# An attention kernel's inner loop and tail: row maxima taken one by one, two sums joined, one head's row scores issued ahead, GpSimd relieved of two sums, one bias moved

## The chip, the cores and the metric

The kernel runs on one core of one Trainium2 chip. The metric is the device time of one execution in microseconds (us), as the median of several runs. The engines named here are PE (TensorE, with PEld for its weight loads), DVE (VectorE), ACT (ScalarE), POOL (GpSimd) and SP (SyncE, which issues DMAs).

## The reference

Eight batches of 512 rows with 512 features, 16 heads of 32. A condition vector per batch is projected with the same weights and added to Q and K; then comes plain softmax attention, and the input is added as a residual. All is float32.

```python
Q, K, V = (split_heads(x @ W.T + b) for W, b in ((Wq, bq), (Wk, bk), (Wv, bv)))
cQ = Q + split_heads(tokens @ Wq.T + bq)        # tokens: one condition row per batch
cK = K + split_heads(tokens @ Wk.T + bk)
attn = softmax(cQ @ cK^T / sqrt(32))
out = x + merge_heads(attn @ V)
```

## The kernel before

**The steps.** The work is cut into T = 32 steps; step `t` is one batch and one group of four heads (`b, g = divmod(t, 4)`). For each step the scores are made twice. *Row scores* (`row_scores`, L641) have 128 query rows on the partitions and 512 keys along the row, one PSUM bank a head; DVE takes each row's maximum from them (`one_max`, L589, for one head; `row_max_of`, L650, for two heads whose banks are neighbours), and ACT makes the exponentials with the maximum as bias and their sum (`denominators`, L701). For two of the four query blocks of a step these exponentials are kept and turned (`turn_kept`, L660 on DVE; `swap_kept`, L682, DMAs on the queues of SP and POOL). For the other two blocks, the *rest*, the transposed scores are made anew: `exponentials_of_rest` first puts the maximum into the bank by a bf16 matmul with ones (L774), then adds the rest scores (L785), and ACT takes the exponential (L795).

**The loop.** `thirds(t)` is called for t = 1 to 28 and works in three parts. At its start it makes the row scores of step t+1, query blocks 1 and 2 (`row_max_aside`, `row_max`): head 0's bank of block 1 is copied aside by ACT (L628) and its maximum taken from there (L637), the other three maxima from the banks. Then PE multiplies step t-1's exponentials by V (`weighted`, L816), and makes one item of the projections of a coming batch (`one_item`). Parts i = 1 and i = 2 each make one half of the rest of step t, the row scores of one block of a later step (block 3 of step t+1, then block 0 of step t+2), and one more item. An odd t makes Q first, Q other, K first; an even t V first, K other, V other. The projections are done with seven block products in place of eight, all in `product` (L461), so each item ends in sums that put the products together: `first_by_others` (Q and K first), `other_products` (Q and K other; L551, L486 on DVE), `first_of_v` (copies by ACT, L1217 and L1218) and `other_shared` (V other; L1202 on ACT, L1204 to L1206 on DVE, L1208 on POOL).

**Order and banks.** PE, ACT, DVE and POOL run in the order in which the code is written; nothing is reordered by a planner on them. The eight PSUM banks go round: `begin` and `released` keep a list of them by the time of their release, and `banks(i)` is the i-th of the list. A matmul that writes a bank waits until the bank's last reader is done. `begin` also sorts a neighbouring pair to the end of a group of four, so that the two last heads can share one maximum.

**Row strips.** Head j lies on partitions 32j to 32j+31, so the four heads' scores use four different strips of 32 rows of TensorE. Projections and the products with V use strips of 32 columns.

**The tail.** From t = 29 on the code is written out. It splits the row maxima of step 30 into three bf16 parts on DVE (`split_max`, L715 to L718), turns them on PE (`transpose_max`, L737), and goes on with `crossed` (L1270, L1273), in which row scores and transposed scores alternate. `bias_residual` (L204) is a POOL sum that adds V's bias to the residual of a step; the tail calls it for steps 31, 29 and 30.

Of the kernel before, what the change touches and what calls it, by code (L numbers as in the profile page):

```python
# [17 lines left out]
def kernel(  # L18
# [38 lines left out]
    nc = tc.nc  # L57
# [451 lines left out]
    def first_by_others(n, b, u, dens, at, last, mixed):  # L509

        one_, two_ = halves(banks(at[0])), halves(banks(at[1]))
        c1, c12, c2, c22 = parts_of(n, b, u)
        product(n, b, u, 1, one_[:, 0])
        product(n, b, u, 7, one_[:, 1])
        product(n, b, u, 6, two_[:, 1])
        product(n, b, u, 2, two_[:, 0], (0,))
        if mixed:
            dens((0, 1))
            nc.scalar.copy(c2, one_)
            dens((2, 3))  # L520
            nc.vector.tensor_tensor(c1, two_, twice(c2[:, 0, :]), ALU.add)
            last()
        else:
            dens((0, 1))
            if mixed is False:
                dens((2, 3))
            if mixed is None:
                dens((2, 3))
                nc.vector.tensor_copy(c2, one_)
                nc.vector.tensor_copy(c1, two_)  # L530
            else:
                nc.scalar.copy(c2, one_)
                nc.scalar.copy(c1, two_)
            last()
            nc.gpsimd.tensor_tensor(c12, c12, c2[:, 0, :], ALU.add)
            nc.gpsimd.tensor_tensor(c22, c22, c12, ALU.add)
            nc.gpsimd.tensor_tensor(c1[:, 0, :], c1[:, 0, :], c2[:, 0, :], ALU.add)
            return
        nc.gpsimd.tensor_tensor(c22, c22, c12, ALU.add)
# [48 lines left out]
    def one_max(t, qc, j, pt):  # L588
        nc.vector.tensor_reduce(  # L589
            nmax[t][:, qc, j : j + 1, 0], pt, AX.X, ALU.max, negate=True  # L590
        )

    def row_max(t, qc, hold=False, w=HG):

        if t >= T:
            return
        open_max(t)
        for j in range(HG):
            row_scores(t, qc, j, banks(w + j))
        if row_of[0] or t < T - 2 or t * NS + qc == T * NS - 1:  # L600
            for j in range(2):
                one_max(t, qc, j, banks(w + j))
        else:
            row_max_of(t, qc, 0, banks(w, 2))
        last, both = [banks(w + 2), banks(w + 3)], banks(w + 2, 2)
        apart = row_of[0] and row_of[0][w + 3] - row_of[0][w + 2] > 1

        def held():
            if apart or hold and t < T - 2:
                for j in range(2):  # L610
                    one_max(t, qc, 2 + j, last[j])
            else:
                row_max_of(t, qc, 1, both)

        if hold:
            return held
        held()
        return nothing
# [4 lines left out]
    def row_max_aside(t, qc):  # L623

        open_max(t)
        for j in range(HG):
            row_scores(t, qc, j, banks(j))
        nc.scalar.copy(spare, banks(0).rearrange("p (c f) -> p c f", f=P))  # L628
        one_max(t, qc, 1, banks(1))
        if row_of[0][3] - row_of[0][2] > 1:  # L630
            for j in (2, 3):
                one_max(t, qc, j, banks(j))
        else:
            row_max_of(t, qc, 1, banks(2, 2))

    def max_aside(t, qc):
        nc.vector.tensor_reduce(nmax[t][:, qc, 0:1, 0], spare, AX.XY, ALU.max, negate=True)  # L637
# [11 lines left out]
    def row_max_of(t, qc, pr, pt):  # L649
        nc.vector.tensor_reduce(  # L650
            nmax[t][:, qc, pr * 2 : pr * 2 + 2, 0], pt, AX.X, ALU.max, negate=True
        )
# [112 lines left out]
            for i in range(2):  # L765
                nc.scalar.activation(e[:, i, :], bank[pr * 2 + i], AF.Exp)

    def exponentials_of_rest(t, half):

        bank = [banks(i) for i in range(HG)]  # L770
        rest = slice(KQ * P, S)
        for j in range(HG):
            r = slice(j * HD, j * HD + 3)
            nc.tensor.matmul(  # L774
                bank[j],
                onesb[r, :],
                maxT[t][r, rest].unsqueeze(1).broadcast_to([3, 2, HS]),
                start=True,
                stop=False,
            )  # L780
        for i in range(2):
            kc = half * 2 + i
            for j in range(HG):
                r = slice(j * HD, (j + 1) * HD)
                nc.tensor.matmul(  # L785
                    bank[j][:, i * HS : (i + 1) * HS],
                    qkT["k", t][r, kc * P : (kc + 1) * P],
                    qkT["q", t][r, rest],
                    start=False,
                    stop=(i == 1),  # L790
                )
        for pr in range(NP):
            e = es[t, half, pr] = store[:, 12 + half * 2 + pr]
            for i in range(2):
                nc.scalar.activation(e[:, i, :], bank[pr * 2 + i], AF.Exp)  # L795

    def times_v(t, kc, pt, chunks=range(NS)):
        b, g = divmod(t, G)
# [330 lines left out]
    def thirds(t, made):  # L1129

        b, r = divmod(t, G)
        of = (t - 1) // G + 1
        begin(0, HG)
        turn_more(t, 0, 0)
        row_max_aside(t + 1, 1)
        max_aside(t + 1, 1)
        row_max(t + 1, 2, False, HG)
        turn_more(t, 0, 1)
        denominators(t + 1, 1, None, (1, 2, 3, 0))
        denominators(t + 1, 2, HG)  # L1140
        weighted(t - 1, banks(0), banks(1), nothing)
        turn_more(t, 0, 2)
        load_blocks()
        one_item(of, *next(made), (2, 3), ignore, nothing)
        released(0, 1, 4, 5, 6, 7, 2, 3)
        for i in (1, 2):
            begin(HG)
            exponentials_of_rest(t, i - 1)
            turn_more(t, i, 0)
            rows = (t + 1, 3) if i == 1 else (t + 2, 0)  # L1150
            row_max(*rows, False, HG)
            turn_more(t, i, 1)
            if i == 1:
                first = range(6 if t + 1 < KEPT[-1] else 3)
                swap_kept(t, 2, first)
                split_max(t + 1)
                turn_max(t + 1)
                swap_kept(t, 2, range(len(first), 6))
            dens = lambda js=range(HG): denominators(*rows, HG, js)
            n, u, kind = next(made)  # L1160
            if kind == "first":
                products(of, n, u, kind, False, dens, nothing, None)
                turn_more(t, i, 2)
            elif n == "v":
                small = nothing
                if t + 1 not in KEPT:
                    small = lambda: transpose_max(t + 1, banks(2), nc.scalar.copy)
                other_shared(of, n, u, dens, (0, 3), small, lambda: turn_more(t, i, 2))
                released(1, 2, 4, 5, 6, 7, 0, 3)
            else:  # L1170
                products(of, n, u, kind, False, dens, nothing, False)
                turn_more(t, i, 2)
            if i == 1:
                aparts[t] = masked(t)
            load_blocks()
            if (t + 1, i) == (KEPT[-1], 1):
                swap_kept(t + 1, 0)
            if i == 2:
                if r == 0:
                    combine_x(b + 1, 1, nc.gpsimd)  # L1180
                load_residual(t + 1)
            else:
                if t > 1:
                    bias_residual(t)
                if r == 0:
                    combine_x(b + 1, 0, nc.gpsimd)
            if i == 2 and t + 1 < KEPT[-1]:
                for move in range(2):
                    swap_kept(t + 1, move)

    def other_shared(b, n, u, dens, at, small, more):

        dens((0, 1))
        one_, two_ = banks(at[0]), banks(at[1])
        product(n, b, u, 4, one_[:, :HS])
        product(n, b, u, 5, one_[:, HS:])
        small()
        product(n, b, u, 2, two_[:, :HS])
        product(n, b, u, 3, two_[:, HS:])
        c1, c12, c2, c22 = parts_of(n, b, u)  # L1200
        m45 = aside[:, 0]
        nc.scalar.copy(m45, halves(one_))  # L1202
        dens((2, 3))
        nc.vector.tensor_tensor(c12, one_[:, HS:], c12, ALU.add)  # L1204
        nc.vector.tensor_tensor(c1[:, 0, :], two_[:, :HS], c2[:, 0, :], ALU.add)
        nc.vector.tensor_tensor(c12, two_[:, HS:], c12, ALU.add)  # L1206
        more()
        nc.gpsimd.tensor_tensor(c2, m45, twice(c22), ALU.add)  # L1208

# [97 lines left out]
    else:  # L1307
        row_max_of(t + 1, 2, 1, banks(HG + 2, 2))
    row_max_of(t + 1, 2, 0, late[0][:, :2, :])
    swap_kept(t, 1)  # L1310
    apart = masked(t - 1)
    aparts[t] = masked(t)
    load_residual(t + 2)
    bias_residual(t + 2)
    swap_kept(t, 2)
    bias_residual(t)
    load_residual(t + 1)
    halves_of(t - 1, banks(0), (1,))
    row_of[0] = [*second[:2], *first[2:], *first]
# [152 lines left out]
```

## Time and profile before

| | |
|---|---|
| runs | 653.80, 654.09, 654.63 us (median 654.09) |
| profiled execution | 656.53 us, span 654.7 us, mean granted TensorE clock 0.997 of full speed |
| PE busy | 647.7 us (99%) |
| DVE busy | 598.4 us (91%) |
| ACT busy | 534.3 us (82%) |
| POOL busy | 428.6 us (65%) |
| loop (t = 1 to 28) | from 66.2 to 606.7 us |

The profile comes from one execution; the span runs from its first to its last instruction. A busy PE need not be PE at its peak, since matmuls are pipelined and one that waits inside can count as busy. Rows of the timeline give start, duration, engine, line, operation, what is written from what, the shape, the count, and in brackets the idle time before and what ended it.

### The profile page before, as it was taken

Reading aid. Unit: us, or ns where it says so; the run is one execution under the profiler, and the core shown is the slowest. Engines: PE = TensorE matmul, PEld = TensorE weight load, DVE = VectorE, ACT = ScalarE, POOL = GpSimd, SP = SyncE. Lnnn points to the kernel's source line nnn. Section 1 sums busy time; section 2 is a strip of 40 time slices with the busy share of each in tenths; the row PEclk is TensorE's granted clock in tenths of the full one; section 3 lists DMA queues with packets and bytes.
Section 4 is the critical chain, followed back from the end, with each engine's and each line's share of the span. In section 5 each row is a group of like instructions: output and inputs, shape, how many; then the busy total and the mean of one; then the engine's idle time right before and its main releaser. Section 6 shows DMA issues by size and latency. Waiting matters only on the chain. (4 is left out here: it accounts for less than half of the span.)

```text
span 654.7 us, 24917 instructions
## 1 busy us (share of the span) xinstructions
PE 647.7 (99%) x9856; PEld 350.3 (54%) x9856; DVE 598.4 (91%) x833; ACT 534.3 (82%) x1364; POOL 428.6 (65%) x679
## 2 busy tenths in 40 slices
PE   9999999999999999999999999999999999999997
PEld 8445555555555555555555555555555555555442
DVE  3799999999999999999999999999999989899877
ACT  2479888889888888988888988888898888898464
POOL 3643656786766786777657786668767676766550
PEclk9999999999999999999999999999999999999999
DMA  7633588889877887877877888788987767797811
GB/s 188 107 49 61 127 170 181 172 167 183 185 154 173 163 183 168 185 179 160 173 173 155 188 181 169 165 172 174 171 187 175 149 148 165 147 170 159 190 34 33
DMA packets 248457, 102.02 MB, mean 156 GB/s; under 512 B 229962, under 2 KB 230474, under 8 KB 248340
## 3 DMA queue, kind: packets, MB, share of 16 engines
q1 hardware_dynamic: 234196, 65.54, 53.8%
q0 software_dynamic: 12384, 33.83, 19.2%
q8 instruction: 78, 1.28, 0.9%
q10 hardware_dynamic: 1760, 1.05, 0.5%
q14 instruction: 39, 0.32, 0.2%
HBM read 19.75 MB, written 8.39 MB: 43 GB/s over the span
## 5 line engine op out<-in xcount | busy, mean ns | idle before, releaser
L701 ACT ACTIVATE store<-psum,nmax 128x512 f32<-128x512 f32 x204 | 140.0, 701 | 36.1 <-DVE nmax L589 26.3
L701 ACT ACTIVATE psum<-psum,nmax 128x512 f32<-128x512 f32 x248 | 164.7, 669 | 3.6 <-DVE nmax L589 3.0
L589 DVE TENSOR_REDUCE nmax<-psum 128x1 f32<-128x512 f32 x225 | 144.5, 679 | 18.9 <-PE psum L641 16.6
L650 DVE TENSOR_REDUCE nmax<-psum 128x2 f32<-128x1024 f32 x125 | 151.5, 1212 | 0.0
L641 PE MATMUL psum<-kT,qT 32*128 32x512 f32 x1024 | 143.2, 619 | 0.0
L795 ACT ACTIVATE store<-psum 128x512 f32<-128x512 f32 x232 | 119.8, 603 | 26.9 <-PE psum L785 26.9
L682 POOL DMA_DIRECT2D store<-store x258 | 128.3, 503 | 18.1 <-DMA store<-store 9.3
L660 DVE STREAM_TRANSPOSE store<-store 128x1024 f32<-128x1024 f32 x116 | 138.9, 1217 | 0.0
L816 PE MATMUL psum<-store,v 128*32 128x256 f32 x1856 | 107.6, 383 | 0.0
L816 PEld LDWEIGHTS psum<-store,v 128*32 128x32 f32 x1856 | 57.2, 110 | 57.5 <-ACT wT_q L628 21.2
L889 POOL TENSOR_TENSOR res<-res,recs 128x512 f32<-128x512 f32 x30 | 31.3, 1045 | 84.5 <-DVE res L888 84.5
L641 PEld LDWEIGHTS psum<-kT,qT 32*128 32x128 f32 x1024 | 56.0, 184 | 35.7 <-issue 19.6
L785 PE MATMUL psum<-qT,kT 32*128 32x256 f32 x928 | 59.9, 373 | 0.0
L701 ACT ACTIVATION_READ_ACCUMULATOR psum<-psum,nmax 128x1 f32 x248 | 52.9, 213 | 0.0
L461 PE MATMUL psum<-wc_v,xc 128*32 128x256 f32 x768 | 47.7, 379 | 0.0
L785 PEld LDWEIGHTS psum<-qT,kT 32*128 32x128 f32 x928 | 45.5, 184 | 4.0 <-issue 0.3
L204 POOL TENSOR_TENSOR xr<-xr,bvs 128x512 f32<-128x512 f32 x30 | 38.5, 1282 | 9.9 <-DMA xr<-in_x_dram 9.8
L461 PE MATMUL psum<-xc,wc_q 128*32 128x256 f32 x720 | 44.5, 379 | 0.0
L461 PE MATMUL psum<-xc,wc_k 128*32 128x256 f32 x720 | 44.5, 379 | 0.0
L701 ACT ACTIVATION_READ_ACCUMULATOR store<-psum,nmax 128x1 f32 x204 | 44.0, 216 | 0.0
L890 POOL TENSOR_TENSOR res<-res,xr 128x512 f32<-128x512 f32 x30 | 38.3, 1278 | 2.4
L461 PE MATMUL psum<-xT,wT_k 128*32 128x256 f32 x480 | 34.5, 382 | 0.0
(195 smaller groups left out, 995.3 us busy)
## 6 DMA issues: line engine op xcount, KB each, us to landing
store<-store SPq DMA_DIRECT2D x264, 128.0 KB, 2.7
store<-store POOLq DMA_DIRECT2D x258, 128.0 KB, 3.6
out_dram<-res SPq DMA_DIRECT2D x122, 64.0 KB, 3.3
xr<-in_x_dram SPq DMA_DIRECT2D x120, 64.0 KB, 2.5
x<-in_x_dram SPq DMA_DIRECT2D x112, 64.0 KB, 3.8
w_q<-in_L_cond_Wq_dram SPq DMA_DIRECT2D x4, 256.0 KB, 3.7
w_v<-in_L_cond_Wv_dram SPq DMA_DIRECT2D x16, 64.0 KB, 2.4
w_k<-in_L_cond_Wk_dram SPq DMA_DIRECT2D x16, 48.0 KB, 2.5
```

Of the source, the lines that this page charges most:

```text
L204: nc.gpsimd.tensor_tensor(xr[t], xr[t], bias, ALU.add)
L461: nc.tensor.matmul(pt[r], still[:, r], moving, start=(kc == kcs[0]), stop=(kc == kcs[-1]))
L589: nc.vector.tensor_reduce(nmax[t][:, qc, j : j + 1, 0], pt, AX.X, ALU.max, negate=True)
L641: nc.tensor.matmul(pt, qkT["q", t][r, qc * P : (qc + 1) * P], qkT["k", t][r, :], start=True, stop=True,)
L650: nc.vector.tensor_reduce(nmax[t][:, qc, pr * 2 : pr * 2 + 2, 0], pt, AX.X, ALU.max, negate=True)
L660: nc.vector.transpose(e, e)
L682: (nc.gpsimd if here else nc.sync).dma_start(to, of)
L701: nc.scalar.activation(to, of, AF.Exp, bias=nmax[t][:, qc, j, :], accum_out=sums[t][:, qc, j, :],)
L785: nc.tensor.matmul(bank[j][:, i * HS : (i + 1) * HS], qkT["k", t][r, kc * P : (kc + 1) * P], qkT["q", t][r, rest], start=False, stop=(i == 1),
L795: nc.scalar.activation(e[:, i, :], bank[pr * 2 + i], AF.Exp)
L816: nc.tensor.matmul(pt[j * HD : (j + 1) * HD, half * HS : (half + 1) * HS], vs[b % 2][:, kc, (g * HG + j) * HD : (g * HG + j + 1) * HD], e, ...
L890: nc.gpsimd.tensor_tensor(y, y, xr.pop(t), ALU.add)
```

## The change

Six things are changed.

1. `first_by_others` with `mixed is None` (K first, in odd thirds): DVE's second operation, which copied the second bank (L530), becomes a sum of that bank and the first product. Two of POOL's three sums (L535, L537) go; the third (L536) stays.
2. `row_max_aside`: heads 1, 2 and 3 always get a maximum of their own; so far heads 2 and 3 shared one where their banks are neighbours.
3. `exponentials_of_rest` is cut into `less_max`, `scores_of_rest` and `rest_leaves`. With the three called one after another the instructions are the same as before.
4. In odd thirds, part 1 (the phase of Q other), `joined` takes the place of `exponentials_of_rest` and the scores of `row_max`: head 1's row scores are issued right behind the maximum matmuls, ahead of the rest scores; the other heads' rest scores and one half of head 1's follow, then the other heads' row scores, then head 1's second half. ACT takes heads 0, 2, 3 and then 1; DVE takes the maximum of head 1 before that of head 0.
5. `other_shared` (V other, even thirds): two DVE sums over 256 columns (L1205, L1206) become one over 512.
6. In the tail the POOL sum `bias_residual(t)` for t = 29 moves up, ahead of two rounds of swaps, two small products and another bias.

```diff
             if mixed is None:
                 dens((2, 3))
                 nc.vector.tensor_copy(c2, one_)
-                nc.vector.tensor_copy(c1, two_)
+                nc.vector.tensor_tensor(c1, two_, twice(c2[:, 0, :]), ALU.add)
+                last()
+                nc.gpsimd.tensor_tensor(c22, c22, c12, ALU.add)
+                return
...
-    def row_max(t, qc, hold=False, w=HG):
+    def row_max(t, qc, hold=False, w=HG, scores=True):
...
-        for j in range(HG):
+        for j in range(HG if scores else 0):
             row_scores(t, qc, j, banks(w + j))
         if row_of[0] or t < T - 2 or t * NS + qc == T * NS - 1:
-            for j in range(2):
+            for j in range(2) if scores else (1, 0):
                 one_max(t, qc, j, banks(w + j))
...
         nc.scalar.copy(spare, banks(0).rearrange("p (c f) -> p c f", f=P))
-        one_max(t, qc, 1, banks(1))
-        if row_of[0][3] - row_of[0][2] > 1:
-            for j in (2, 3):
-                one_max(t, qc, j, banks(j))
-        else:
-            row_max_of(t, qc, 1, banks(2, 2))
+        for j in (1, 2, 3):
+            one_max(t, qc, j, banks(j))
...
+    def joined(t, half, rows):
+
+        sooner, others = 1, (0, 2, 3)
+        less_max(t)
+        row_scores(*rows, sooner, banks(HG + sooner))
+        scores_of_rest(t, half, 0, others)
+        scores_of_rest(t, half, 1, others)
+        scores_of_rest(t, half, 0, (sooner,))
+        for j in others:
+            row_scores(*rows, j, banks(HG + j))
+        scores_of_rest(t, half, 1, (sooner,))
+        rest_leaves(t, half, (*others, sooner))
...
-            exponentials_of_rest(t, i - 1)
-            turn_more(t, i, 0)
             rows = (t + 1, 3) if i == 1 else (t + 2, 0)
-            row_max(*rows, False, HG)
+            if i == 1 and r % 2 == 1:
+                joined(t, i - 1, rows)
+                turn_more(t, i, 0)
+                row_max(*rows, False, HG, False)
+            else:
+                exponentials_of_rest(t, i - 1)
+                turn_more(t, i, 0)
+                row_max(*rows, False, HG)
...
         nc.vector.tensor_tensor(c12, one_[:, HS:], c12, ALU.add)
-        nc.vector.tensor_tensor(c1[:, 0, :], two_[:, :HS], c2[:, 0, :], ALU.add)
-        nc.vector.tensor_tensor(c12, two_[:, HS:], c12, ALU.add)
+        v = vs[b % 2].rearrange("p k (h f) -> p (k h) f", h=2)
+        nc.vector.tensor_tensor(c1, halves(two_), v[:, u * 2 + 1 : u * 2 + 5 : 3, :], ALU.add)
...
     row_max_of(t + 1, 2, 0, late[0][:, :2, :])
+    bias_residual(t)
     swap_kept(t, 1)
     apart = masked(t - 1)
     aparts[t] = masked(t)
     load_residual(t + 2)
     bias_residual(t + 2)
     swap_kept(t, 2)
-    bias_residual(t)
     load_residual(t + 1)
```

The new functions that `joined` calls:

```python
    def less_max(t):
        for j in range(HG):
            r = slice(j * HD, j * HD + 3)
            nc.tensor.matmul(
                banks(j),
                onesb[r, :],
                maxT[t][r, KQ * P :].unsqueeze(1).broadcast_to([3, 2, HS]),
                start=True,
                stop=False,
            )

    def scores_of_rest(t, half, i, js=range(HG)):
        kc = half * 2 + i
        for j in js:
            r = slice(j * HD, (j + 1) * HD)
            nc.tensor.matmul(
                banks(j)[:, i * HS : (i + 1) * HS],
                qkT["k", t][r, kc * P : (kc + 1) * P],
                qkT["q", t][r, KQ * P :],
                start=False,
                stop=(i == 1),
            )

    def rest_leaves(t, half, js):
        e = store[:, 12 + half * 2 : 14 + half * 2].rearrange("p c i s -> p (c i) s")
        for pr in range(NP):
            es[t, half, pr] = e[:, pr * 2 : pr * 2 + 2]
        for j in js:
            nc.scalar.activation(e[:, j], banks(j), AF.Exp)
```

More of the change, by code (lines that the diff above doesn't have):

```diff
@@ L766, in exponentials @@
                 nc.scalar.activation(e[:, i, :], bank[pr * 2 + i], AF.Exp)
-    def exponentials_of_rest(t, half):
-        bank = [banks(i) for i in range(HG)]
-        rest = slice(KQ * P, S)
+    def less_max(t):
         for j in range(HG):
@@ L774, in exponentials_of_rest @@
             nc.tensor.matmul(
-                bank[j],
+                banks(j),
                 onesb[r, :],
-                maxT[t][r, rest].unsqueeze(1).broadcast_to([3, 2, HS]),
+                maxT[t][r, KQ * P :].unsqueeze(1).broadcast_to([3, 2, HS]),
                 start=True,
@@ L780, in exponentials_of_rest @@
             )
-        for i in range(2):
[L782 to L795, printed above, removed]
+    def scores_of_rest(t, half, i, js=range(HG)):
+        kc = half * 2 + i
+        for j in js:
+            r = slice(j * HD, (j + 1) * HD)
+            nc.tensor.matmul(
+                banks(j)[:, i * HS : (i + 1) * HS],
+                qkT["k", t][r, kc * P : (kc + 1) * P],
+                qkT["q", t][r, KQ * P :],
+                start=False,
+                stop=(i == 1),
+            )
+    def rest_leaves(t, half, js):
+        e = store[:, 12 + half * 2 : 14 + half * 2].rearrange("p c i s -> p (c i) s")
+        for pr in range(NP):
+            es[t, half, pr] = e[:, pr * 2 : pr * 2 + 2]
+        for j in js:
+            nc.scalar.activation(e[:, j], banks(j), AF.Exp)
+    def exponentials_of_rest(t, half):
+        less_max(t)
+        for i in range(2):
+            scores_of_rest(t, half, i)
+        rest_leaves(t, half, range(HG))
+    def joined(t, half, rows):
+        sooner, others = 1, (0, 2, 3)
+        less_max(t)
+        row_scores(*rows, sooner, banks(HG + sooner))
[6 more added lines that the diff above has]
+        rest_leaves(t, half, (*others, sooner))
     def times_v(t, kc, pt, chunks=range(NS)):
```

## The prediction

> **What bounds the kernel now.** I first read how busy the engines are over two neighbouring calls of `thirds`, t = 11 (odd, 259.40 to 278.57 us) and t = 12 (even, 278.57 to 297.95); the last row of that table of windows sums the two:
>
> ```profile
> sum 38.55, PE 38.55 PEld 21.27 DVE 36.54 ACT 33.59 POOL 28.58; mean PE 19.28 PEld 10.64 DVE 18.27 ACT 16.80 POOL 14.29
> ```
>
> PE is busy all the 38.55 us, DVE is idle for 2.01 of it, ACT and GpSimd for more. So the loop lasts as long as PE's stream. But a matmul that waits for its bank can count as busy, so next I read PE's timeline by starts:
>
> ```profile
> 259.40 2.08 PE L641 MATMUL psum<-kT,qT 32*128 32x512 f32 x16
> 261.42 3.66 PE L816 MATMUL psum<-store,v 128*32 128x256 f32 x64
> ```
> ```profile
> 268.32 1.03 PE L785 MATMUL psum<-qT,kT 32*128 32x256 f32 x16
> 269.19 1.03 PE L641 MATMUL psum<-kT,qT 32*128 32x512 f32 x8
> 270.14 1.07 PE L461 MATMUL psum<-xc,wT_q 128*32 128x256 f32 x16
> ```
> ```profile
> 274.39 1.09 PE L641 MATMUL psum<-kT,qT 32*128 32x512 f32 x8
> 275.41 1.07 PE L461 MATMUL psum<-xT,wT_k 128*32 128x256 f32 x16
> ...
> 287.91 1.19 PE L641 MATMUL psum<-kT,qT 32*128 32x512 f32 x8
> 289.04 1.07 PE L461 MATMUL psum<-xc,wT_k 128*32 128x256 f32 x16
> ...
> 293.29 1.14 PE L641 MATMUL psum<-kT,qT 32*128 32x512 f32 x8
> 294.36 1.07 PE L461 MATMUL psum<-wT_v,xc 128*32 128x256 f32 x16
> ```
>
> Each matmul is recorded as two passes, so x8 are the row scores of four heads. From their start to the next group it takes 0.95 us at 269.19, but 1.02 at 274.39, 1.13 at 287.91 and 1.07 at 293.29: the same work with 0.07, 0.18 and 0.12 of waiting. The two sets at 259.40 take 2.02. The rest scores (268.32 to 269.19, as many columns) need 0.87 a set where no other tile shape follows, so 0.08 of the 0.95 is the change of shape. Two sets then need 0.87 + 0.95 and about 0.1 for the change of shape ahead of them: 1.92 to 1.94, so 0.08 of the 2.02 is waiting; I count the same at the start of an even third. An odd third thus waits 0.08 + 0.07 = 0.15 us, an even one 0.08 + 0.18 + 0.12 = 0.38. Fourteen of each hold 7.4 us, and that is all the loop's edits can win.
>
> Then the end of the program. Here PE really stands still:
>
> ```profile
> 619.91 0.49 PE L737 MATMUL psum<-identb,split 128*128 128x128 bf16 x4 [1.44 <-DVE split L718]
> 620.33 1.94 PE L816 MATMUL psum<-store,v 128*32 128x256 f32 x16
> 622.20 1.22 PE L641 MATMUL psum<-kT,qT 32*128 32x512 f32 x2
> 622.21 0.61 PE L1270 MATMUL psum<-maxT,onesb 3*128 3x512 bf16 x2
> 622.61 1.03 PE L1273 MATMUL psum<-qT,kT 32*128 32x512 f32 x2
> 623.21 0.73 PE L641 MATMUL psum<-kT,qT 32*128 32x512 f32 x2
> ```
>
> **The change part by part.** *V's last sums joined* (even thirds, last item). DVE before, the weight load of the next third's row scores that waits for them (PEld), and a sum of the joined one's size elsewhere:
>
> ```profile
> 259.54 0.42 DVE L1205 TENSOR_TENSOR v<-psum,v 128x256 f32<-128x256 f32 x1 [0.20 <-PE psum L461]
> 259.88 0.41 DVE L1206 TENSOR_TENSOR v<-psum,v 128x256 f32<-128x256 f32 x1
> ```
> ```profile
> 260.35 0.31 PEld L641 LDWEIGHTS psum<-kT,qT 32*128 32x128 f32 x7 [0.23 <-DVE v L1206]
> ```
> ```profile
> L555 DVE TENSOR_TENSOR v<-psum,v 128x512 f32<-128x512 f32 x2 | 1.4, 678 | 0.0
> ```
>
> Both sums already wait for the whole bank, so the joined one starts at 259.54 too and ends 0.68 later, at 260.22 instead of 260.29. It frees the bank 0.07 sooner, and the odd third's first 0.08 shrinks to about 0.01 (bounds: 0 to 0.08 won).
>
> *Maxima one by one.* ACT stops waiting for the maximum of the pair, which DVE makes in 1.21 us:
>
> ```profile
> 281.12 1.21 DVE L650 TENSOR_REDUCE nmax<-psum 128x2 f32<-128x1024 f32 x1
> ```
> ```profile
> 282.36 0.69 ACT L701 ACTIVATE store<-psum,nmax 128x512 f32<-128x512 f32 x1 [0.35 <-DVE nmax L650]
> ```
> ```profile
> 287.52 0.41 ACT L1218 COPY v<-psum 128x256 f32<-128x256 f32 x1
> ```
>
> ACT runs without another gap from 282.36 to the copy that ends at 287.93. That copy frees the bank that PE needs at 287.91, hence the 0.18. With ACT 0.35 sooner it ends at 287.58, and the 0.18 goes. Late next is DVE's chain behind the same scores: it makes K, which the row scores at 293.29 read.
>
> ```profile
> 291.64 1.51 DVE L486 SCALAR_TENSOR_TENSOR kT<-psum,tok,kT 128x512 f32<-128x512 f32 x2
> ```
>
> K is done at 293.15, 5.24 after the scores began at 287.91, through three maxima and three sums without a stop, but for PE's products: the last two sums take 1.51 here and 1.40 in the odd third (row at 272.91 below), so 0.11 of the 5.24 is waiting for PE. PE came at 293.29, 5.38 behind the start, so K was done 0.14 before that, and the scores waited 0.12 all the same (weights are still to be loaded). With the 0.18 gone PE comes after 5.20 and K after 5.13: 0.07 before, so the wait grows by 0.07 to 0.19. Of the 0.18 some 0.10 stays won (bounds 0 and 0.18).
>
> *One head's row scores ahead* (odd thirds, Q's phase). DVE and ACT around it:
>
> ```profile
> 268.98 0.67 DVE L371 STREAM_TRANSPOSE xT<-x 128x512 f32<-128x512 f32 x1
> 270.24 1.29 DVE L589 TENSOR_REDUCE nmax<-psum 128x1 f32<-128x512 f32 x2 [0.59 <-PE psum L641]
> ```
> ```profile
> 272.91 1.40 DVE L486 SCALAR_TENSOR_TENSOR qT<-psum,tok,qT 128x512 f32<-128x512 f32 x2
> ```
> ```profile
> 267.22 0.67 ACT L701 ACTIVATE psum<-psum,nmax 128x512 f32<-128x512 f32 x1
> ```
>
> PE does not wait here today, so nothing is won on the spot. Head 1's scores would start at 268.32 and end one set later, 0.87, rather than two. DVE, done with the transpose at 269.65, need not idle 0.59. The maxima end some 0.5 sooner, but DVE then waits for PE's Q products, and Q's second sum, which ended at 274.31, ends about 0.07 sooner. That is what the scores at 274.39 wait for: their 0.07 goes. (Two single maxima take 1.29 here against 1.21 for a pair: the 0.08 that the one-by-one maxima cost DVE in every third is less than this idle time.) Price: the four heads use four row strips, and each strip gets the same columns as before, so the stream is as long if strips run apart. The rows at 622.20 to 623.21 show that they do: the code issues both passes of L641 first, yet L1273 starts on other strips at 622.61, ahead of L641's second pass at 623.21. The new wait is head 1's for its bank, with all the rest scores queued behind it. By the lists of `begin` and `released`, in twelve of the fourteen odd thirds this bank is the one that the exponential of 267.22 frees at 267.89, 0.43 ahead of 268.32; in two it is freed by the copy behind that. I take 0, with bounds of 0 (the columns are the same) and 0.2 a third (my estimate if it were the copy everywhere).
>
> *K's first sum in place of a copy.* L530 starts when PE's product ends, not when DVE is free:
>
> ```profile
> 278.78 0.69 DVE L530 COPY kT<-psum 128x512 f32<-128x512 f32 x1 [0.31 <-ACT store L701]
> ```
>
> A sum from PSUM of this size takes 678 ns (L555), the copy 0.69: no difference, and the even third's first 0.08 stays (bounds -0.01 and +0.05, the price if it runs as long as L486's 0.75). GpSimd loses two sums an odd third, which nobody waits for: it idles 9.97 of the 38.55 us. Its swap DMAs queued behind them go out earlier; they are needed a third later.
>
> *Loop:* an odd third falls from 0.15 to 0.01 of waiting, an even one from 0.38 to 0.28: (0.14 + 0.10) x 14 = 3.4 us. The bounds above make it 0.34 x 14 = 4.8 at best and 0.25 x 14 = 3.5 lost at worst.
>
> *The bias moved.* It costs where it goes and where it was:
>
> ```profile
> 611.31 0.55 POOL L682 DMA_DIRECT2D store<-store  x1 [2.43 <-DMA store<-store]
> ```
> ```profile
> 617.21 0.49 POOL L682 DMA_DIRECT2D store<-store  x1 [0.63 <-DMA store<-store]
> 617.72 1.27 POOL L204 TENSOR_TENSOR xr<-xr,bvs 128x512 f32<-128x512 f32 x1
> ```
> ```profile
> 617.38 1.68 DVE L715 CAST split<-nmax 128x16 bf16<-128x16 f32 x1
> ```
> ```profile
> 616.67:620.08 3.41, 1.97 (x19) 1.00 0.93 212
> 620.08:623.49 3.41, 3.41 (x30) 0.50 0.05 9
> ```
>
> From 608.88 to 611.31 GpSimd waits for a swap, so the 1.27 us of bias fits there free: the six swap DMAs, two masks and the last bias that it is moved past start no later. If that wait were gone, they would be 1.27 late. DVE's cast of 16 numbers takes 1.68 us because it cannot end before GpSimd is through: it ends at 619.06, 0.07 after the bias (618.99). Without the bias it would end that far behind the DMA issue, 617.70 + 0.07 = 617.77: 1.29 sooner. The casts that follow, PE's transpose and everything behind them move up by 1.29 of the 1.44 that PE stood still.
>
> The second windows row has PE at half clock (0.50) for the 3.41 us right behind the stretch in which PE was busy only 1.97. All of it is PE's work, 1.71 us at full clock. With the standstill down to 0.15 I expect full clock there: 1.6 more, a little kept for waits that come up (bounds 0 and 1.71). The tail gives 1.3 + 1.6 = 2.9.
>
> **Sum.** 3.4 + 2.9 = 6.3 us. The profiled execution took 656.53 us (span 654.7), 2.44 over the median of the runs; 656.53 - 6.3 = 650.2 there, 654.09 - 6.3 = 647.8 on the median.
>
> **The rivals.** *Half clock stays:* then the tail gives 1.3, and 649.4 results. For it: one trace can't show that the standstill is the cause. Against it: the stretch before, with the same kind of work, has the full clock (1.00). The Trainium skill, TensorE: Matmul & The Clock Gate (Part 1: The HAM clock gate), lets the clock fall after an idle window of about 3.4 us; by that rule 1.44 us is not enough and this rival holds, but the row shows the fall behind 1.44. Chance 0.12.
>
> *The loop's waits only move* (DVE has 2.01 us in 38.55 to spare, and its K chain is level with PE): the tail alone, 651.2. Chance 0.15.
>
> *Slower: the head put ahead holds the others.* If PE started matmuls strictly in the order of issue, passes included, a set of 0.87 is two passes of 0.43, and a half-width pass 0.22. Head 1 starts at 0 and 0.43, seven rest scores follow in steps of 0.22 to 1.94, three row scores to 3.23, and head 1's last rest score ends at 3.66, against 1.73 for two sets now. That is 1.93 in each of 14 odd thirds, 27 us, and 675. It decides from 0.54 us an odd third on (6.3 + 1.3 over 14). Against it stand the rows from 622.20 on. The same page of the Trainium skill (Part 3: Packing small matmuls, The mechanism) calls matmuls strictly first in, first out, which would give this rival; the trace disagrees there. Chance 0.08, smaller holds of 0.2 to 0.5 a third (650.6 to 654.8) 0.07.
>
> **How the numbers follow.** Forecast 0.58: 647.8. At best the loop gives 4.8 and the tail 3.0, which is 646.3; the runs before spread by 0.8, so the range begins at 645.9. It ends at 651.5, beyond both partial cases, and leaves out the slower rival and most of the smaller holds. 0.2% is 1.3 us, about what a measurement of this kernel tells from none: faster (under 652.8) 0.58 + 0.12 + 0.15 + 0.02 = 0.87, same 0.04, slower 0.09.
>
> **What would show it.** Right: odd thirds near 19.03 us and even ones near 19.28 (start of one double set to the next); scores at 0.95 in Q's phase and after it; ACT's 0.35 gone; DVE's first maximum right behind the transpose; L715 under 0.5 us, no half-clock window. Wrong: Q's phase on PE longer than before, a new wait on head 1's bank, or K later than 5.2 us behind its scores.

## The result, and the profile after

The kernel after took 651.37 us (median of 6 runs, 650.46 to 652.76) beside 654.36 for the kernel before (6 runs): the ratio is 0.9952, with a 95% interval of 0.9937 to 0.9967. Two more sets of runs, each on one chip with the kernel before beside it, gave 0.9945 (0.9932 to 0.9959) and 0.9947 (0.9932 to 0.9962). The change wins 3.0 to 3.4 us, about half of the 6.3 that were forecast. The profiled execution took 652.28 us (span 650.4), against 656.53 (654.7) before: 4.25 less, more than the medians show.

The table of windows, t = 11 and t = 12 (columns as before: us, then busy time and instructions of PE, PEld, DVE, ACT, GpSimd, then granted clock, DMA share, GB/s):

```profile
259.30:278.34 19.04, 19.04 (x316) 10.86 (x312) 18.46 (x25) 16.55 (x44) 13.06 (x22) 1.00 0.83 174
278.34:297.60 19.26, 19.26 (x316) 10.46 (x312) 18.17 (x25) 17.02 (x47) 13.97 (x23) 1.00 0.76 168
sum 38.30, PE 38.30 PEld 21.33 DVE 36.64 ACT 33.56 POOL 27.04; mean PE 19.15 PEld 10.66 DVE 18.32 ACT 16.78 POOL 13.52
```

This pair of thirds takes 38.30 us instead of 38.55; forecast were 19.03 and 19.28, measured are 19.04 and 19.26. PE's timeline shows where, each set read from its start to the next group's:

```profile
259.30 2.02 PE L640 MATMUL psum<-kT,qT 32*128 32x512 f32 x16
261.25 3.66 PE L839 MATMUL psum<-store,v 128*32 128x256 f32 x64
...
274.23 1.03 PE L640 MATMUL psum<-kT,qT 32*128 32x512 f32 x8
275.18 1.07 PE L461 MATMUL psum<-xT,wT_k 128*32 128x256 f32 x16
...
278.34 2.06 PE L640 MATMUL psum<-kT,qT 32*128 32x512 f32 x16
280.33 3.66 PE L839 MATMUL psum<-store,v 128*32 128x256 f32 x64
...
287.67 1.03 PE L640 MATMUL psum<-kT,qT 32*128 32x512 f32 x8
288.63 1.07 PE L461 MATMUL psum<-xc,wT_k 128*32 128x256 f32 x16
...
292.02 1.03 PE L784 MATMUL psum<-qT,kT 32*128 32x256 f32 x16
292.94 1.14 PE L640 MATMUL psum<-kT,qT 32*128 32x512 f32 x8
294.01 1.07 PE L461 MATMUL psum<-wT_v,xc 128*32 128x256 f32 x16
```

The odd third's double set takes 1.95 (2.02 before), the scores behind Q's sums 0.95 (1.02), those of the even third's first item 0.96 (1.13). The even third's double set still takes 1.99. At the K chain the rest scores (292.02 to 292.94) now take 0.92 instead of 0.87, and the row scores 1.07 as before. Both are counted from start to start, so a later start of the row scores lengthens the row ahead of them, and the wait for K went from 0.12 to 0.17.

DVE's timeline, the two sums that replaced others and the first maximum in Q's phase:

```profile
259.44 0.69 DVE L1234 TENSOR_TENSOR v<-psum,v 128x512 f32<-128x512 f32 x1 [0.27 <-PE psum L461]
...
268.87 0.67 DVE L371 STREAM_TRANSPOSE xT<-x 128x512 f32<-128x512 f32 x1
269.46 1.30 DVE L592 TENSOR_REDUCE nmax<-psum 128x1 f32<-128x512 f32 x2
...
278.54 0.69 DVE L530 TENSOR_TENSOR kT<-psum,kT 128x512 f32<-128x512 f32 x1 [0.24 <-ACT store L700]
```

The maximum (L592) stands right behind the transpose, without the 0.59 of idle time. Both sums take 0.69.

The end of the program, on DVE, GpSimd and PE:

```profile
616.08 0.20 DVE L714 CAST split<-nmax 128x16 bf16<-128x16 f32 x1
```
```profile
607.69 1.28 POOL L204 TENSOR_TENSOR xr<-xr,bvs 128x512 f32<-128x512 f32 x1
609.67 1.04 POOL L681 DMA_DIRECT2D store<-store  x2 [0.69 <-DMA store<-store]
```
```profile
615.57 1.61 PE L640 MATMUL psum<-kT,qT 32*128 32x512 f32 x8
617.13 0.40 PE L736 MATMUL psum<-identb,split 128*128 128x128 bf16 x4
```

The bias lies in GpSimd's idle time, the cast takes 0.20 us, and PE runs into its transposes without a gap. The one new thing in the waits is this, late in the loop:

```profile
499.22 0.40 PE L771 MATMUL psum<-maxT,onesb 3*128 3x512 bf16 x4 [1.13 <-DMA maxT<-split]
```

PE stood 1.13 us for one DMA transpose of the maxima.

**The two spans in three pieces.** The last call of `thirds` ends where the tail's double set of row scores begins:

```profile
66.24 2.48 PE L641 MATMUL psum<-kT,qT 32*128 32x512 f32 x16
606.73 2.08 PE L641 MATMUL psum<-kT,qT 32*128 32x512 f32 x16
```
```profile
66.66 2.53 PE L640 MATMUL psum<-kT,qT 32*128 32x512 f32 x16
605.33 2.18 PE L640 MATMUL psum<-kT,qT 32*128 32x512 f32 x16
```

Before (first fence) the 28 calls took 540.49 us and the tail 654.7 - 606.73 = 48.0. After, 538.67 and 45.1. By this pair the tail gave 2.9, as forecast, and the loop 1.8 instead of 3.4. The timed runs say something else of both.

### The profile page after: what moved, and what is told of

Its sections match the earlier page's. It is cut to its first block, busy times and chain, and to the rows that moved or that the text cites. A ratio compares the mean times of both kernels' runs of the same rounds, so it can differ in the third digit from the quotient of the medians.

```text
span 650.4 us, 24900 instructions
## 1 busy us (share of the span) xinstructions
PE 643.4 (99%) x9856; PEld 352.8 (54%) x9856; DVE 598.4 (92%) x846; ACT 534.3 (82%) x1364; POOL 409.6 (63%) x651
## 5 line engine op out<-in xcount | busy, mean ns | idle before, releaser
L592 DVE TENSOR_REDUCE nmax<-psum 128x1 f32<-128x512 f32 x279 | 177.0, 677 | 11.0 <-PE psum L640 6.2
L640 PE MATMUL psum<-kT,qT 32*128 32x512 f32 x1024 | 150.8, 612 | 0.0
L649 DVE TENSOR_REDUCE nmax<-psum 128x2 f32<-128x1024 f32 x98 | 118.9, 1213 | 0.0
L640 PEld LDWEIGHTS psum<-kT,qT 32*128 32x128 f32 x1024 | 56.8, 183 | 36.4 <-issue 18.0
L784 PE MATMUL psum<-qT,kT 32*128 32x256 f32 x928 | 71.9, 373 | 0.0
L784 PEld LDWEIGHTS psum<-qT,kT 32*128 32x128 f32 x928 | 53.1, 184 | 4.8 <-issue 0.3
```

Source lines behind the costliest of these rows:

```text
L592: nc.vector.tensor_reduce(nmax[t][:, qc, j : j + 1, 0], pt, AX.X, ALU.max, negate=True)
L640: nc.tensor.matmul(pt, qkT["q", t][r, qc * P : (qc + 1) * P], qkT["k", t][r, :], start=True, stop=True,)
L649: nc.vector.tensor_reduce(nmax[t][:, qc, pr * 2 : pr * 2 + 2, 0], pt, AX.X, ALU.max, negate=True)
L784: nc.tensor.matmul(banks(j)[:, i * HS : (i + 1) * HS], qkT["k", t][r, kc * P : (kc + 1) * P], qkT["q", t][r, KQ * P :], start=False, stop= ...
```

## The experiments

Theory A: the tail's 2.9 is what one disturbed execution lost; ordinary runs lose less there. Theory B: the loop is shorter as forecast, but maxima that come late by DMA take part of it back. Theory C: the head put ahead costs in some thirds what it wins behind Q. The rival to all is that the loop's waits only move. Every ratio below is to the kernel before on the same chip.

**e1, the bias alone** (on the kernel before):

```diff
     row_max_of(t + 1, 2, 0, late[0][:, :2, :])
+    bias_residual(t)
     swap_kept(t, 1)
...
     swap_kept(t, 2)
-    bias_residual(t)
```

> The kernel before with the bias of the tail moved and nothing else. Theory A (the half clock behind PE's standstill is an accident of the profiled run and seldom there in an ordinary run of the kernel before): only the standstill goes, 1.3 us, so about 653.1 against 654.4, ratio 0.998. The forecast's sum (standstill and half clock, 2.9): about 651.5, ratio 0.9956. In the trace by either: the cast of 16 numbers under 0.5 us, no idle time of 1.44 ahead of PE's transposes, full clock there; thirds as before.

Measured: 653.51 us against 654.21; ratio 0.9990 (0.9981 to 0.9999), so 0.7 us, between 0.1 and 1.2. The forecast's 2.9 is excluded; theory A holds, with an even smaller sum than it named. The cast is short and PE's gap is gone, as forecast:

```profile
617.71 0.20 DVE L715 CAST split<-nmax 128x16 bf16<-128x16 f32 x1
```
```profile
618.76 0.40 PE L737 MATMUL psum<-identb,split 128*128 128x128 bf16 x4
```

The loop of this trace, which has no edit, takes 540.75 us (540.49 in the trace of before).

**e2 and e9, the loop's edits alone** (the kernel after with the bias put back), on two chips:

> The kernel after with the bias back at its old place: the loop's four edits alone. The forecast's sum: 3.4 us less than before, about 651.0, ratio 0.9948. Theory B (the thirds are shorter as forecast, but SyncE's transposed maxima come later from third to third until PE waits for one, about 1 us each time): 1.7 less, about 652.7, ratio 0.9974. The rival of the prediction that the loop's waits only move: 654.2, ratio 1. In the trace: odd thirds 19.05 to 19.11, even ones 19.27; by theory B at least one wait of PE for maxT of 0.5 us or more.

> The loop's four edits alone once more (the bias of the tail at its old place), now on the same chip as the kernel after, so that the two differ by the bias alone. Theory A (the tail's term was read from an execution with a long standstill): 0.5 to 0.9 above the kernel after, and in the trace a standstill ahead of PE's transposes that is another one than 1.44 us, at full clock. The forecast: 2.9 above.

Measured: e2 651.85 against 654.21, ratio 0.9967 (0.9955 to 0.9979), 2.2 us (1.4 to 2.9). e9 651.71 against 654.54, ratio 0.9951 (0.9936 to 0.9967), 3.2 us (2.2 to 4.2), and 0.5 above the kernel after beside it (e10); the runs of these two overlap (650.73 to 652.17 and 650.84 to 651.80), so the 0.5 alone can't be told from nothing. The rival that waits only move is out. Five traces have the bias at its old place. Of the cast of 16 numbers (DVE's row) and PE's gap behind it (PE's row, the bracket) they tell this, in the order e2, e12, e4, e9; the kernel before had 1.68 and 1.44:

```profile
616.26 1.40 DVE L714 CAST split<-nmax 128x16 bf16<-128x16 f32 x1
618.51 0.40 PE L736 MATMUL psum<-identb,split 128*128 128x128 bf16 x4 [1.15 <-DVE split L717]
```
```profile
615.47 1.44 DVE L711 CAST split<-nmax 128x16 bf16<-128x16 f32 x1
617.75 0.40 PE L733 MATMUL psum<-identb,split 128*128 128x128 bf16 x4 [1.19 <-DVE split L714]
```
```profile
616.86 0.80 DVE L715 CAST split<-nmax 128x16 bf16<-128x16 f32 x1
618.51 0.40 PE L737 MATMUL psum<-identb,split 128*128 128x128 bf16 x4 [0.56 <-DVE split L718]
```
```profile
614.26 0.48 DVE L714 CAST split<-nmax 128x16 bf16<-128x16 f32 x1
615.58 0.40 PE L736 MATMUL psum<-identb,split 128*128 128x128 bf16 x4 [0.23 <-DVE split L717]
```

The gap is anything from 0.23 to 1.44. In all five the cast ends 0.06 to 0.08 behind GpSimd's bias, so the gap follows how late the bias starts. In the three traces with long gaps GpSimd had waited for the landing of a swap right ahead of the bias (0.63 us in before, 0.54 in e2, 0.59 in e12); in e4 and e9 it had not. And behind e2's gap there is no half clock (the granted clock is the third column from the right):

```profile
617.11:618.51 1.40, 0.25 (x2) 0.00 (x1) 1.23 (x5) 0.00 (x0) 0.48 (x1) 1.00 1.19 241
618.51:621.92 3.41, 3.41 (x40) 1.60 (x40) 3.41 (x6) 1.74 (x4) 0.37 (x1) 1.00 0.05 8
```

The tails, worked out as above (span less the start of the last double set), are 46.3 in e2, 46.2 in e12, 45.6 in e4 and 45.3 in e9. With the bias moved, the traces of e1, after and e7 give 44.9 to 45.1.

**e3 and e4, the head put ahead taken away, and alone.** e3 is the kernel after with the odd thirds' old order, e4 the kernel before with the new order:

```diff
-            if i == 1 and r % 2 == 1:
+            if False:
                 joined(t, i - 1, rows)
```

> The kernel after with the rest scores of the odd thirds in their old order (no head's row scores ahead), all else as after. The forecast: the 0.07 us of the scores behind Q's sums comes back in 14 odd thirds, 1.0 us, so about 652.4. Theory C (the head put ahead costs 0.07 us in every second odd third, in its own phase, and wins 0.06 behind Q): 14 x 0.06 - 7 x 0.07 = 0.4 us, so about 651.8. If it is worth nothing: 651.4. In the trace: the rest scores and row scores of Q's phase 2.05 us in all odd thirds, and DVE's first maximum 0.5 us or more behind its transpose.

> The kernel before with one head's row scores ahead in Q's phase of the odd thirds (and the sums, the maxima set aside and the bias as before). The forecast: 0.07 us in 14 odd thirds, 1.0 us, so about 653.4. Theory C: 0.4 us, about 654.0. Strict order of issue would have made it 27 us longer, which the kernel after already excludes. In the trace: the scores behind Q's sums at 0.95 to 0.97 us in the odd thirds, Q's phase 0.07 longer in the thirds t = 5, 9, 13, 17, 21, 25 alone.

Measured: e3 651.39 against 654.21, ratio 0.9960 (0.9948 to 0.9972); e4 654.14, ratio 1.0003 (0.9992 to 1.0014). Alone the edit wins at most 0.5 us; the forecast's 1.0 is excluded. Where it loses shows in the trace of the kernel after, at the end of Q's phase at t = 11 and t = 13, and in PE's weight loads there:

```profile
269.66 0.37 PE L784 MATMUL psum<-qT,kT 32*128 32x256 f32 x1
269.97 1.07 PE L461 MATMUL psum<-xc,wT_q 128*32 128x256 f32 x16
```
```profile
307.96 0.37 PE L784 MATMUL psum<-qT,kT 32*128 32x256 f32 x1
308.34 1.07 PE L461 MATMUL psum<-xc,wT_q 128*32 128x256 f32 x16
```
```profile
269.97 0.14 PEld L461 LDWEIGHTS psum<-xc,wT_q 128*32 128x32 f32 x5 [0.34 <-ACT store L798]
```
```profile
308.31 0.19 PEld L461 LDWEIGHTS psum<-xc,wT_q 128*32 128x32 f32 x8 [0.38 <-POOL qT L538]
```

From the last score to Q's products it is 0.31 at t = 11 but 0.38 at t = 13. At t = 11 the weight load waits for ACT's exponential of the rest scores, whose bank the products take over. At t = 13 the record has a semaphore event of its own ahead of the load (51 ns, at 308.2), and the load names GpSimd's L538, which had ended at 308.17, before the load began. So the 0.07 looks like the price of a second wait ahead of the load; no run tests that by itself. The same 0.06 to 0.07 stands in all six thirds t = 5, 9, ... 25 of e4 and in no other odd third. In e3 the odd thirds have no such 0.07, but DVE's first maximum waits 0.53 again and the scores behind Q take 1.02:

```profile
274.40 1.09 PE L640 MATMUL psum<-kT,qT 32*128 32x512 f32 x8
275.42 1.07 PE L461 MATMUL psum<-xT,wT_k 128*32 128x256 f32 x16
```

So theory C fits the traces: 0.07 won 14 times, 0.07 lost six times, about 0.5 us. By time it is less clear: e4 shows no gain at all (0.5 is the end of its interval), and theory C's price of 651.8 for e3 can't be told from 651.4 by these runs.

**e12, the maxima one by one** (on the kernel before; it is the diff's last hunk in `row_max_aside`):

> The kernel before with the maxima beside the head set aside taken one by one, and nothing else. The forecast's term: 0.18 won and 0.08 given back at the K chain in 14 even thirds, 1.4 us, about 652.7. By the traces of the kernel after (0.164 won, 0.062 given back): 1.4 too. The rival that the wait only moves: no change. In the trace: even thirds 0.10 shorter, ACT's 0.35 gone; odd thirds as before.

Measured: 652.9 against 654.54; ratio 0.9976 (0.9967 to 0.9986), 1.6 us. Even thirds 19.28 instead of 19.38, odd ones 19.17 as before. The trace's loop is 1.5 shorter.

**e5 to e8, e10 and e11: late maxima.** e5 and e10 are the kernel after again. The others move the residual's loads (four DMAs a third), which stand ahead of SyncE's swaps: e6 issues them on GpSimd behind its swaps, e7 on SyncE behind its swaps, e8 is e6 without the head put ahead, and e11 is e6 with the last load back on SyncE.

```diff
-                load_residual(t + 1)
...
                 for move in range(2):
                     swap_kept(t + 1, move)
+            if i == 2:
+                load_residual(t + 1, nc.gpsimd)   # e7: nc.sync
```

> The kernel after once more, beside the three that follow and the kernel before. About 651.4 by every theory. Theory B (SyncE's transposed maxima land later from third to third until PE waits for one): a wait of PE for maxT, or a lead of its landing over its use of under 1 us, between t = 17 and t = 23.

> The kernel after with the four loads of the residual of each third issued by GpSimd behind its own swaps, and no longer by SyncE ahead of its. Theory B: SyncE's queue is 3.7 us shorter a third, maxT lands 4 us or more ahead of its use in every third, PE's waits for it go, and with them 0.8 to 1.2 us: about 650.4. The rival (the late maxima are rare, and the rest of the loop's shortfall lies elsewhere): the same as after, 651.4. If GpSimd's 2 us of issuing make its sums late instead: 652 or more.

> The kernel after with the four loads of the residual still on SyncE, but behind its swaps. By theory B the swaps go out 3.7 us sooner, and what hangs on them (GpSimd's swaps, its split of the maxima) with them, while SyncE's queue is no shorter: if the swaps' landing is what makes maxT late, as good as with the loads on GpSimd, 650.4; if the length of SyncE's queue is, no better than after, 651.4, and a bias that waits for its load may cost some more.

> As the kernel with the residual's loads on GpSimd, and without the head put ahead. By the thirds of the runs so far (0.064 us won behind Q in 14 odd thirds, 0.071 lost in its own phase in six) the head is worth 0.47 us where nothing else is late: 0.5 above the one with it, about 650.9. If the head put ahead is worth nothing or harms: the same or less.

> The kernel after, beside the others of this set and the kernel before: 650.6 to 651.4, 3.0 to 3.4 below before. Tail (from the start of the last call's scores to the end) 45.08 as in the traces so far.

> The kernel after with the residual's loads issued by GpSimd inside the loop alone; the last one, for which GpSimd's moved bias waited 3.24 us, stays on SyncE. The loop was 537.30 us with all of them on GpSimd, 537.38 with them behind SyncE's swaps, and 537.82 to 538.68 in the two traces of the kernel after; the tail should be back at 45.1. Theory B: no wait of PE for maxT, 0.3 to 1.2 below the kernel after, about 650.2. If late maxima are rare in ordinary runs: the same as the kernel after.

Measured, on one chip: e5 650.59 (to 652.71), e6 653.23, e7 650.71 (to 651.74), e8 653.84, before 653.95. On another: e10 651.22, e11 651.55, before 654.54. In the traces e6, e7 and e11 do to the loop what theory B says: no wait for maxT, and the loop is 537.3 to 537.4 us (603.83 - 66.45 in e7):

```profile
66.45 2.48 PE L640 MATMUL psum<-kT,qT 32*128 32x512 f32 x16
603.83 2.18 PE L640 MATMUL psum<-kT,qT 32*128 32x512 f32 x16
```

That doesn't show that moving the loads did it: e9, with the loads at their old place, has no late maximum either, and its loop takes 537.36 us.

```profile
66.15 2.48 PE L640 MATMUL psum<-kT,qT 32*128 32x512 f32 x16
603.51 2.18 PE L640 MATMUL psum<-kT,qT 32*128 32x512 f32 x16
```

And e7's median is that of e5, and e11's is no lower than e10's. e6 gave its gain back in the tail: GpSimd's moved bias waited for the load that GpSimd now issued late, and the swaps waited behind the bias.

```profile
612.26 1.27 POOL L204 TENSOR_TENSOR xr<-xr,bvs 128x512 f32<-128x512 f32 x1 [3.24 <-DMA xr<-in_x_dram]
```

In e11 PE waits in the tail instead. The profile names ACT, but in e10 PE entered the same products while ACT was still in these exponentials, so what released it is not settled:

```profile
619.61 0.64 PE L839 MATMUL psum<-store,v 128*32 128x256 f32 x8 [0.95 <-ACT store L1318]
```

So late maxima are real in single executions (1.13 us in the trace of after, 0.9 in e2's), yet moving the loads lowers no median: theory B may explain part of the spread between runs, but it is not shown to explain the shortfall. e8 minus e6 is 0.6, which agrees with theory C's 0.5 for the head. No variant beat the kernel after measurably.

## Why the prediction was wrong

**What failed is the tail's term**, 1.3 + 1.6 = 2.9 us, which measured 0.7 (e1, between 0.1 and 1.2) and 0.5 (e9 beside e10). The mechanism was right: the cast does not end before GpSimd is through with the bias, and without the bias it takes 0.20. The size was that of one execution. The half clock behind the gap was in that one alone: the granted clock of 61 recorded executions of the kernel before in the later sets is 0.998 to 1.000, where this one has 0.997 (half clock for 3.41 of 654.7 us costs 0.0026 of the mean), and e2 and e12 kept the full clock behind gaps of 1.15 and 1.19. The gap itself was the longest of five.

The prediction held the evidence. It noted that the profiled execution lay 2.44 over the median, and then took the same 6.3 off the profile and off the median. If the loop (540.49), the beginning (66.24) and the 1.83 outside the span were those of an ordinary run, the median of 654.36 leaves 45.8 for the tail, not 48.0. By this count moving the bias brings 45.8 - 45.1 = 0.7, which is what e1 measured; with e1's loop of 540.75 it brings 0.5. The four other traces with the bias at its old place have tails of 45.3 to 46.3.

**The loop's term**, 3.4, is 3.1 in a trace in which nothing is late (540.49 - 537.36 of e9), and 2.2 and 3.2 in the timed runs of e2 and e9. So of the 2.9 to 3.3 us that are missing from the 6.3, the tail's term is 2.2 to 2.4, and the head put ahead about 0.5; what is left is within the spread of the runs. By its parts:
- V's sums joined: 0.07 an odd third, as forecast (2.02 to 1.95). It was not run alone, but e12 and e4, which lack it, keep 2.00 to 2.02 from t = 3 on, and e3 has 1.94 to 1.95. The tail's own double set got longer, 2.11 instead of 2.02, once.
- Maxima one by one: 0.17 won (1.13 to 0.96) and 0.05 given back at the K chain (0.12 to 0.17; forecast 0.18 and 0.07). e12 measured 1.6 for a forecast of 1.4.
- One head ahead: 0.07 won behind Q, as forecast. The price was set at 0 with a bound of 0.2, and the suspected wait was at the head's own bank. The wait came elsewhere, at the products that follow, 0.07 in six thirds. Half a microsecond is left of the 1.0 by the traces.
- K's first sum: nothing at the place that was forecast, the even third's double set (2.01 to 1.99).
- In the trace of the kernel after, the even thirds t = 24, 26 and 28 take 19.17 to 19.19, some 0.09 less than the others, 0.27 in all; this was not forecast. There the weight load of the K chain's scores begins 0.06 us behind the end of K's last sum, elsewhere 0.12, and the semaphore event of its own that stands ahead of the load elsewhere is missing. So part of the 0.12 that the prediction put down to weights still to be loaded looks like the second wait of theory C. e3, e2 and e9 have the short thirds, e12 and e4 have not, so they need V's or K's sums; which of the two stays open, as neither was run alone.

The rival of strict order is out: row scores (L640) start among rest scores (L784), and Q's phase from 267.92 to 269.97 takes 2.05, as long as before.

```profile
268.15 0.38 PE L784 MATMUL psum<-qT,kT 32*128 32x256 f32 x1
268.15 0.59 PE L640 MATMUL psum<-kT,qT 32*128 32x512 f32 x1
268.16 0.80 PE L784 MATMUL psum<-qT,kT 32*128 32x256 f32 x6
268.59 0.58 PE L640 MATMUL psum<-kT,qT 32*128 32x512 f32 x1
```

By its time the result is that of the rival "the loop's waits only move" (651.2), but not for its reason: the loop won 2.2 to 3.2 and the tail nearly nothing, the reverse of what that rival says. Nor is it the rival "half clock stays": in the ordinary run there was no half clock to stay.

Left open: by what rule the clock fell behind 1.44 us in one execution. The Trainium skill, TensorE: Matmul & The Clock Gate (Part 1: The HAM clock gate), asks for an idle window of about 3.4 us; e2 and e12 agree with that, the trace of before does not.

The traces narrow it down. Each of the 14 ends with a fall to half clock. In the trace of before this is at 654.21, which is 34.13 us behind the fall at 620.08, ten times 3.413, and the half clock there lasted 3.41. I divided every trace into stretches of 3.413 us, counted back from its own last fall. Half clock follows the stretches in which PE was busy 1.98 us or less: 616.66 to 620.08 in before, and the last one of every trace (at most 1.58). Full clock follows all others: the lowest have 2.09 (in after, near the end), 2.22 (e12, with its gap of 1.19) and 2.26 (e2, with its gap of 1.15). So a limit between 1.98 and 2.09 us of busy time in 3.413 fits all 14 traces. By it a gap of 1.44 lowers the clock if it lies within one stretch, and a gap of 1.19 does not. This is a reading of traces, and no run was made to test it.

Also open is a hold of 0.35 us ahead of one even third's scores, at t = 16 in the trace of before and t = 6 in that of after.

## What to carry to other kernels

When the profiled execution lies above the median, find where the excess lies before summing: a gain counted there is partly a gain that ordinary runs never lost. A stall behind a DMA's landing is a distribution, not a number; here it was 0.23 to 1.44 us in five executions, while most thirds from t = 3 on agree within 0.02 us between traces of the same loop. Take such a term at the length that the median leaves for it, not at the length of the one trace, and where work is moved to another queue, look at what waits behind it a stage later.

## What the runs showed that I had not expected

- The waits between compute engines repeat almost exactly: the pair t = 11 and 12 took the same 38.30 us in the traces of the kernel after, of e7 and of e10.
- One DMA transpose of the maxima came too late although it was issued 5.2 us before PE was ready for it (498.09); PE went on at 499.22, 6.3 behind the issue:

```profile
492.88 1.25 SPq L726 DMA_TRANSPOSE maxT<-split  x1
```

- The profiled execution of the kernel after was 0.9 above the first median, and that of e5 was the slowest of its five runs (652.71 beside 650.23 to 650.83); that of e7 and e9 was not. One trace can't be taken for the ordinary run in either direction.
